# Running a single-head cross attention and the ternary feed-forward layer behind it in one loop over chunks

## The chip, the cores and the metric

The kernel runs on one core of a Trainium2 chip. The metric is device time in microseconds (us) of one execution; for the kernel before it is the median of three timed runs, 3519.1 us (3512.54 to 3522.86). The profile comes from one further execution, which the hardware profiler recorded; it has a time of its own, given below.

## The reference

A decoder of four layers, each made of a self-attention-like step, a cross-attention step and a feed-forward step, twelve steps in all. Each step adds its result to the stream `x` and normalises the sum. `x` is 128 batches x 64 positions x 128 numbers, 8192 tokens in float32; the context has the same shape. The first layer is:

```python
x = _layernorm(x + _L0_attn_ref(x, ...))            # a top-2 mixture of experts
x = _layernorm(x + _L0_xattn_ref(x, ctx_1024, ...)) # single-head cross attention
x = _layernorm(x + _L0_ffn_ref(x, ...))             # ternary feed-forward
```

The two steps that the change touches compute

```python
q, k, v = x @ Wq + bq, ctx @ Wk + bk, ctx @ Wv + bv
xattn   = softmax(q k^T / sqrt(128)) v                      # 64 x 64 weights per batch

ternary(w) = w + stop_gradient(clip(round(w / s), -1, 1) - w),  s = max(mean(|w|), 1e-8)
h       = gelu(x @ ternary(W1)^T + b1)                       # exact gelu, 512 wide
ffn     = h @ ternary(W2)^T + b2
```

and the layernorm is `(x - mean) / sqrt(var + 1e-5)` over the 128 numbers of a token. The fourth step, which follows them, is a differential attention with 8 heads.

## The kernel before

**Tiling.** The stream is cut into 16 chunks of 512 tokens (8 batches each), a chunk into 4 tiles of 128 tokens. `X[c]`, 128 partitions x 4 x 128, stays in SBUF in float32 from the first step to the last. Whatever TensorE multiplies with a weight it needs turned, so a chunk is transposed on TensorE into PSUM and copied by ScalarE to a tile `xT` (128 features x 512 tokens).

**Order of the work.** The kernel's text issues operations in program order. The framework's scheduler makes one list for each engine from them when the kernel is built, and adds the semaphore waits. It keeps most of the program order, and takes an operation forward where nothing it depends on holds it back: the clearing of `VX` below, late in the text, stands first on GpSimd. On the chip an engine works its list from front to back: an instruction that waits holds all behind it. So the order of the calls in a loop, with what the scheduler moved, is the order on every engine. `tc.issue_after` keeps an operation from being moved ahead of a given one. Buffers come from named rings: `bank` gives one of three PSUM banks in turn, `wide` (and the scores' tile, of the same tag) one of five, `work("r")` one of three SBUF buffers, `work("xT")`, `work("tmp")`, `work("tab")` and `work("h")` one of two. Whoever takes a buffer waits until its last reader is done.

**Step 1, the mixture of experts,** has written the experts' outputs to DRAM in the order of the experts. `moe_done(c)` brings them back for a chunk with indirect DMAs that GpSimd issues (L805, 8 for a chunk), and VectorE and ScalarE add them, and normalise (`L369` and the lines around it, `L378`). Chunks 5 to 15 are brought back inside the loop of step 2, each some chunks ahead of its use.

**Step 2, `xattn_single`,** runs five functions in each turn of its loop, each for another chunk:

- `scores(i+1)`: q k^T per batch into `s_ps`; the maximum on VectorE (L1001 to L1002 and after), four `Exp` on ScalarE (L1005), sum and reciprocal on VectorE.
- `turned_weights(i)`: the exponentials are transposed (a `bank`), copied by ScalarE to `p1T`.
- `projections(i+2)`: q (L940) and its copy with bias on ScalarE (L945), k likewise, then v: a product of bfloat16 rows puts the bias into the bank (L981, `bv`, the bias split into three bfloat16 parts so that the sum is exact to float32), eight pairs of small products add to it (L986), and ScalarE copies it out.
- `values(i)`: weights times v into `y0` and `y1` (L1026); VectorE scales and adds `X` (tile `r1`), then `layernorm(..., on_act=True)`: statistics, `rsqrt` and the tile `lns` on VectorE, the last step (`x <- r * y + lns`) on ScalarE, L378.
- `sources(i+3)`: `moe_done`, the transposed context (`turned_context`), the transposed `X[i+3]`.

**Step 3, `ffn_ternary`,** first makes the ternary weights (`tern`: `Abs` on ScalarE, a sum through TensorE, then six operations on VectorE for each of two halves). Then `pipelined(range(NC), hidden, output)` calls `hidden(c)` one chunk ahead of `output(c)`. `hidden` transposes `X[c]`, adds the second bias to `X[c]` on GpSimd (`with_bias`, the copy `xb`), multiplies (L1072, four products into `wide`) and applies `Gelu` on ScalarE (L1074) to `hT`. `output` multiplies `hT` with the second weight (L1082, 16 products into a `bank`), and `add_norm` adds `xb` and normalises; the last step of this layernorm is on GpSimd, L380.

**What comes after.** `attn_diff` begins with the constant tiles `VX[0]` and `VX[1]`, which GpSimd clears and fills with a mask (L1114 and L1116, `G.memset` and `G.tensor_copy`). Nothing else uses those tiles before, so GpSimd does that within the first 10 us of the kernel. In `attn_diff` GpSimd rotates q and k (L1352) and masks copies of them for the heads (L1127, `eb`), and TensorE starts the scores `s_ps` with these.

Of the kernel before, what the change touches and what calls it, by code (L numbers as in the profile page):

```python
# [12 lines left out]
F32 = mybir.dt.float32  # L13
# [9 lines left out]
P = 128  # L23
B, S, D = 128, 64, 128
NTOK = B * S
TPC = 4
# [208 lines left out]
def tile_decoder(ctx: ExitStack, tc: tile.TileContext, a, out):  # L235
# [22 lines left out]
    def work(tag, shape=(P, 512), name=None, dt=F32):  # L258

        width, bufs = SPACES[tag]  # L260
        t = space.tile([P, width], F32, tag=tag, name=name or tag, bufs=bufs)
        n = math.prod(shape[1:])
        t = t if dt == F32 else t.bitcast(dt)
        t = t[: shape[0], :n]
        if len(shape) > 2:
            ax = "abcd"[: len(shape) - 1]
            t = t.rearrange(f"p ({' '.join(ax)}) -> p {' '.join(ax)}", **dict(zip(ax[1:], shape[2:])))
        return t
# [100 lines left out]
        V.tensor_scalar(v, mv[:, :, 1], LN_EPS, None, ALU.add)  # L369
        return mv  # L370

    def ln_apply(c, r, mv, y, store=False, on_act=False):
        if on_act:
            s = sm.tile([P, TPC], F32, tag="lns", name="lns")
            V.scalar_tensor_tensor(s, mv[:, :, 0], -1.0, y, ALU.mult, ALU.mult)
        for t in range(TPC):
            if on_act:
                A.activation(X[c][:, t, :], r[:, t, :], AF.Identity, bias=s[:, t : t + 1], scale=y[:, t : t + 1])  # L378
            else:
                G.tensor_scalar(X[c][:, t, :], r[:, t, :], mv[:, t, 0:1], y[:, t : t + 1], ALU.subtract, ALU.mult)  # L380
        if store:
            nc.sync.dma_start(out=out_v[c], in_=X[c])

    def layernorm(c, r, store=False, on_act=False):

        v = sm.tile([P, TPC], F32, tag="lnv", name="lnv")
        mv = ln_stats(r, v)
        ln_apply(c, r, mv, rsqrt(v, TPC, "ln"), store, on_act)

    def with_bias(c, name):  # L390

# [545 lines left out]
    def projected(w, srcT, name, bias=None):  # L937
# [7 lines left out]
            A.activation(t, ps, AF.Identity, bias=bias)  # L945
        return t


    def xattn_single():
        w = W[1]  # L950
        scale = 1.0 / math.sqrt(D)

        st = {}

        rest = work("tmp", (P, D), "bvrest")
        V.tensor_copy(rest, row("l0xbv"))
        bv = work("tab", (P, 2, P), "bvparts", BF16)
        part = work("tmp", (P, D), "bvpart", BF16)
        V.memset(bv[:, 0, :], 1.0)
        for k in range(3):  # L960
            V.tensor_copy(part, rest)
            if k == 0:
                V.tensor_scalar(bv[:, 1, :], part, ident[:, 0:1], None, ALU.mult)
            else:
                V.scalar_tensor_tensor(bv[:, 1, :], part, ident[:, k : k + 1], bv[:, 1, :], ALU.mult, ALU.add)
            if k < 2:
                V.tensor_tensor(rest, rest, part, ALU.subtract)
        ring = work("e", (P, 4, TPC, D), "v1")

        def sources(c):  # L970
# [4 lines left out]
        def projections(c):  # L975
            s = st[c]
            s["q"] = projected(w[:, 0, :], s["xT"], "qT", col("l0xbq"))
            s["k"] = projected(w[:, 1, :], CTX[c], "kT", col("l0xbk"))

            v = bank("v1_ps")  # L980
            mm(v.rearrange("p (n d) -> p n d", n=4), bv[:32, 0, :], bv[:32, 1, None, :].to_broadcast([32, 4, D]), start=True, stop=False, skip_group_check=True)  # L981
            for f in range(2):
                for j in range(2):
                    for i in range(2):
                        b = 4 * f + 2 * i + j
                        mm(  # L986
                            v[i * S : (i + 1) * S, (2 * f + j) * D : (2 * f + j + 1) * D], CTX[c][:, b * S : (b + 1) * S], w[:, 2, :],
                            start=False, stop=True, skip_group_check=True,
                        )
            s["v"] = ring[:, c % 4]  # L990
            A.copy(s["v"], v.rearrange("p (n d) -> p n d", n=4))
# [41 lines left out]
            layernorm(c, r, on_act=True)  # L1033


        for i in range(-3, NC):
            for step, c in ((scores, i + 1), (turned_weights, i), (projections, i + 2), (values, i), (sources, i + 3)):
                if 0 <= c < NC:
                    step(c)


    def ffn_ternary():
        w = W[2]
        wt = work("tab", (P, 2, FK, P), "tern")
        for n in range(2):
            src = w[:, 4 * n : 4 * n + 4, :].rearrange("p k m -> p (k m)")
# [12 lines left out]

            V.tensor_scalar(df, df, 12582912.0, None, ALU.add)  # L1060
            V.tensor_scalar(df, df, 12582912.0, None, ALU.subtract)
            V.tensor_tensor(df, df, src, ALU.subtract)
            V.tensor_tensor(df, df, src, ALU.add)

        def hidden(c):
            xT = transposed(X[c], "xT")
            xb = with_bias(c, "l0fb2")
            hT = work("h", (P, FK, 512), "hT")
            for k in range(0, FK, 2):
                ps = [wide("h_ps") for _ in range(2)]  # L1070
                for j in range(2):
                    mm(ps[j], wt[:, 0, k + j, :], xT, start=True, stop=True)  # L1072
                for j in range(2):
                    A.activation(hT[:, k + j, :], ps[j], AF.Gelu, bias=col("l0fb1")[:, k + j : k + j + 1])  # L1074
            return hT, xb

        def output(c, state):
            hT, xb = state
            y = bank("y")
            for t in range(TPC):  # L1080
                for k in range(FK):
                    mm(y[:, t * P : (t + 1) * P], hT[:, k, t * P : (t + 1) * P], wt[:, 1, k, :], start=(k == 0), stop=(k == FK - 1))  # L1082
            add_norm(c, y, xb)

        pipelined(range(NC), hidden, output)


    half = const.tile([P, 816], BF16, tag="half", name="half")
# [3 lines left out]
    idh = half[:, 0:128].rearrange("p (n q) -> p n q", n=2)  # L1092
    identh = const.tile([P, P], BF16, tag="identh", name="identh")
    V.tensor_copy(identh, ident)
    VX = [const.tile([P, BPC * 8 * 34], F32, tag=f"vx{n}", name=f"vx{n}") for n in range(2)]

    def rows32(t, g):
        return t[32 * g : 32 * g + 32]
# [784 lines left out]
    def ffn_switch():  # L1883
# [4 lines left out]
            pass  # L1888

    steps = [  # L1890
        moe_top2, xattn_single, ffn_ternary, attn_diff, xattn_causal, ffn_routed,
        attn_alibi, xattn_padded, ffn_conv, attn_scan, xattn_masked, ffn_switch,
    ]
    seen = None
    for n, step in enumerate(steps):
        load_weights(n + 1)

        with tc.issue_after(seen) if seen else nullcontext():
            seen = step()
# [16 lines left out]
```

## Time and profile before

| | |
|---|---|
| timed runs, median of three | 3519.1 us (3512.54 to 3522.86) |
| profiled execution, its own time | 3278.03 us |
| its span, first to last instruction | 3276.3 us |
| granted TensorE clock, mean over the span | 0.946 |
| TensorE (PE) busy | 2882.3 us, 88% |
| weight load (PEld) busy | 2115.1 us, 65% |
| VectorE (DVE) busy | 1973.2 us, 60% |
| ScalarE (ACT) busy | 1614.1 us, 49% |
| GpSimd (POOL) busy | 1521.4 us, 46% |

Busy times are sums over the whole span; they don't say which engine holds up the others in a given stretch. Around the change the same execution reads, in us of busy time:

| stretch | what runs | PE | DVE | ACT | POOL | clock |
|---|---|---|---|---|---|---|
| 410 to 440 (30) | first gathers, start of step 2 | 17.1 | 12.3 | 13.4 | 21.7 | 0.81 |
| 440 to 500 (60) | step 2 with gathers | 42.1 | 46.8 | 37.3 | 46.3 | 0.81 |
| 500 to 527 (27) | the same, to the last gather | 20.5 | 20.8 | 19.0 | 20.6 | 0.80 |
| 527 to 566 (39) | step 2 without gathers | 31.4 | 31.0 | 31.5 | 4.6 | 0.96 |
| 566 to 579 (13) | end of step 2, ternary weights | 5.1 | 12.5 | 6.7 | 0.0 | 0.60 |
| 579 to 711 (132) | step 3, start of step 4 | 129.4 | 66.8 | 58.8 | 69.5 | 0.99 |

Step 2's first product of turned context stands at 408.45 us, its first `values` at 428.1; step 3's first hidden product at 578.3, its last output product ends at 700.2; the first `s_ps` of step 4 stands at 711.35.

In the lines of a timeline the columns are: start in us, duration in us, engine, line of the program, operation, output<-inputs by the program's names, shapes, and xN where N instructions in a row are drawn together; a bracket gives the idle time ahead and what ended it.

### The profile page before, as it was taken

The numbers are of one execution on the slowest core, as the hardware profiler recorded it, in microseconds if no ns is written. First come the engines' busy times: TensorE is split into PE (matmuls) and PEld (weight loads), VectorE is DVE, ScalarE is ACT, GpSimd is POOL, SyncE is SP. The second block draws the span as 40 slices with busy tenths as digits, with TensorE's granted clock in tenths as the row PEclk, the third lists the DMA queues.
The fourth block names the chain that finished last, engine by engine and source line by source line (L and its number), as shares of the span: only waits on it lengthen the run. The fifth ranks groups of instructions, "written<-read, shape, count | busy, mean of one in ns | idle before, by whom it ended". The sixth has DMA issues, their size and how long they took to land. (4 is left out here: it accounts for less than half of the span.)

```text
span 3276.3 us, 110323 instructions
## 1 busy us (share of the span) xinstructions
PE 2882.3 (88%) x47184; PEld 2115.1 (65%) x47184; DVE 1973.2 (60%) x7074; ACT 1614.1 (49%) x3106; POOL 1521.4 (46%) x1548
## 2 busy tenths in 40 slices
PE   5999967999987999999999989998888569998993
PEld 3888834666665777766677767774444336776793
DVE  3733267557777666433256656666778886666246
ACT  3544457445543565333355545643444555654553
POOL 4477473454555344311234445556566322446154
PEclk9999988999998999999999989989988789998997
DMA  5578710000002000000000000000000000001684
GB/s 142 160 214 248 220 52 28 8 1 3 3 3 76 19 4 4 6 1 1 5 11 4 4 5 4 4 13 1 1 1 2 9 1 16 18 15 46 181 266 147
DMA packets 142459, 159.23 MB, mean 49 GB/s; under 512 B 16720, under 2 KB 118096, under 8 KB 141968
## 3 DMA queue, kind: packets, MB, share of 16 engines
q1 hardware_dynamic: 128064, 123.65, 12.7%
q0 software_dynamic: 13184, 27.03, 3.2%
q8 instruction: 370, 6.06, 0.7%
q10 hardware_dynamic: 720, 1.50, 0.1%
q14 instruction: 121, 0.99, 0.1%
HBM read 121.44 MB, written 30.67 MB: 46 GB/s over the span
## 5 line engine op out<-in xcount | busy, mean ns | idle before, releaser
L1183 DVE TENSOR_REDUCE m<-s_ps 128x8 f32<-128x512 f32 x640 | 397.5, 683 | 144.4 <-PE s_ps L1411 50.8
L1232 ACT ACTIVATE e<-t_ps 128x512 f32<-128x512 f32 x640 | 330.0, 601 | 150.7 <-PE t_ps L1225 150.2
L380 POOL TENSOR_SCALAR x<-xb,lnmv,ln_y 128x128 f32<-128x128 f32 x304 | 238.6, 797 | 267.5 <-DVE ln_y L345 267.5
L1250 PE MATMUL av_ps<-vx,e 128*64 128x18 f32 (+1 forms) x10240 | 341.3, 216 | 5.6 <-issue 5.3
L1250 PEld LDWEIGHTS av_ps<-vx,e 128*64 128x64 f32 x10240 | 322.9, 140 | 25.9 <-issue 18.7
L1127 POOL TENSOR_SCALAR eb<-qT,small 128x512 f32<-128x512 f32 x80 | 131.2, 1640 | 431.5 <-ACT qT L943 200.9
L774 ACT ACTIVATE hT<-h_ps,aux 128x256 f32<-128x256 f32 x496 | 206.6, 470 | 208.4 <-PE h_ps L772 102.3
L1213 PE MATMUL t_ps<-eb,kT 32*64 32x128 f32 x10240 | 281.3, 285 | 4.4 <-DVE m L1183 2.2
L805 POOL DMA_INDIRECT got<-l_rout,pli x192 | 194.4, 1012 | 148.7 <-issue 57.7
L772 PE MATMUL h_ps<-ebT,rw 128*128 128x256 f32 x992 | 241.2, 387 | 8.6 <-DMA rw<-in_l0w_dram 4.5
L785 PEld LDWEIGHTS yg<-rw,hT 128*128 128x128 f32 x1984 | 241.8, 192 | 6.4
L1213 PEld LDWEIGHTS t_ps<-eb,kT 32*64 32x64 f32 x10240 | 198.1, 132 | 71.1 <-DVE m L1183 25.6
L785 PE MATMUL yg<-rw,hT 128*128 128x128 f32 x1984 | 242.1, 276 | 0.0
L1175 PE MATMUL s_ps<-eb,qT 32*64 32x256 f32 x5120 | 217.5, 399 | 20.8 <-POOL eb L1127 9.8
L786 DVE TENSOR_TENSOR yo<-yg,aux 128x256 f32<-128x256 f32 x124 | 52.6, 424 | 267.5 <-PE yg L785 264.4
L1255 DVE RECIPROCAL rc<-av_ps 128x32 f32<-128x32 f32 (+1 forms) x192 | 61.7, 321 | 240.7 <-PE av_ps L1250 240.3
L772 PEld LDWEIGHTS h_ps<-ebT,rw 128*128 128x128 f32 x992 | 182.8, 194 | 31.1 <-DVE ebT L760 6.3
L747 POOL DMA_INDIRECT aux<-in_x_dram,plt x156 | 159.9, 1025 | 56.9 <-issue 26.8
L1125 ACT ACTIVATE eb<-qT,small 128x512 f32<-128x512 f32 x160 | 106.8, 715 | 129.3 <-POOL qT L1352 124.1
L380 POOL TENSOR_SCALAR x<-r,lnmv,ln_y 128x128 f32<-128x128 f32 x68 | 54.4, 813 | 225.0 <-DVE ln_y L345 225.0
L1127 POOL TENSOR_SCALAR eb<-kT,small 128x512 f32<-128x512 f32 x80 | 145.9, 1823 | 22.1 <-ACT kT L945 11.3
L1175 PEld LDWEIGHTS s_ps<-eb,qT 32*64 32x64 f32 x5120 | 114.3, 134 | 60.2 <-issue 15.2
(429 smaller groups left out, 6414.5 us busy)
## 6 DMA issues: line engine op xcount, KB each, us to landing
rw<-in_l0w_dram SPq DMA_DIRECT2D x78, 512.0 KB
rw<-in_l3w_dram SPq DMA_DIRECT2D x46, 512.0 KB
l_rout<-yo SPq DMA_DIRECT2D x124, 128.0 KB
aux<-xd SPq DMA_DIRECT2D x46, 128.0 KB
aux<-in_l0b_dram SPq DMA_DIRECT2D x78, 66.0 KB
xd<-vx SPq DMA_DIRECT2D x5, 1024.0 KB
x<-in_x_dram SPq DMA_DIRECT2D x16, 256.0 KB
cin<-in_ctx_dram SPq DMA_DIRECT2D x16, 256.0 KB
```

The costliest lines, as they stand in the source:

```text
L380: G.tensor_scalar(X[c][:, t, :], r[:, t, :], mv[:, t, 0:1], y[:, t : t + 1], ALU.subtract, ALU.mult)
L747: s.gather = G.indirect_dma_start(out=eb[:, i, :], out_offset=None, in_=x[:, :], in_offset=bass.IndirectOffsetOnAxis(ap=tokens[:, 2 * g + ...
L772: s.pe = mm(ps[:, j * GR : (j + 1) * GR], w1[:, (k + j) * P : (k + j + 1) * P], ebT, start=True, stop=True)
L774: s.act_ins = A.activation(hT[k + j], ps[:, j * GR : (j + 1) * GR], s.act, bias=v[:, k + j : k + j + 1])
L785: s.pe = mm(y[:, i * P : (i + 1) * P], hT[k][:, i * P : (i + 1) * P], w2[:, k, :], start=(k == 0), stop=(k == FK - 1))
L805: s.gather = G.indirect_dma_start(out=got[i][k][:, t, :], out_offset=None, in_=s.rout[b][:, :], in_offset=bass.IndirectOffsetOnAxis(ap=whe ...
L1127: ins = (G if h == 2 else V).tensor_scalar(dst, x, mine, None, ALU.mult)
L1175: mm(ps[g][j * S : (j + 1) * S, u * 256 : (u + 1) * 256].rearrange("p (h k) -> p h k", h=4), rows32(s["q"], g)[:, b], rows32(s["eb"], g)[: ...
L1183: last = V.tensor_reduce(s["m"][:, g, 2 * hf : 2 * hf + 2, :].rearrange("p t h -> p (t h)"), ps[g].rearrange("p (n k) -> p n k", k=S), AX. ...
L1213: mm(ps[g][i * S : (i + 1) * S].rearrange("p (a u j q) -> p a u j q", u=2, a=2, j=2)[:, :, u, j, :], rows32(s["k"], g)[:, b], rows32(s["eb ...
L1232: last = A.activation(e[:, g, :], ps[g], AF.Exp, scale=scale)
L1250: mm(av[j * S : (j + 1) * S, 8 * (u - u0) + n, :], ev[:, n // 2, n % 2, u, j, :], vx[:, 2 * (2 * hf + u) + j, n, :], start=True, stop=True,)
```

## The change

Steps 2 and 3 become one loop. `ffn_ternary` as a function of its own is gone; its weights, `hidden` and `output` stand in `xattn_single`, and the entry in the list of steps becomes `None` (the weights of the step after are still loaded at that place). In a turn the calls are now `scores(i+1)`, `turned(i-1)`, `turned_weights(i)`, `projections(i+2)`, `hidden(i-1)`, `values(i)`, `sources(i+3)`, `output(i-1)`; `turned` is the transposing that `hidden` did itself. The two halves of the ternary weights are made after the first and the second turn (`i` = -3 and -2).

With it go four smaller edits. The second bias is no longer added to `X` on GpSimd: `output` starts its bank with the product of bfloat16 rows that v had, made by a helper `bias_rows`, and `added(c, y)` adds `X[c]` itself. The layernorm after the ffn is ended on VectorE for chunks 0 to 7 and on GpSimd for the others. `hT` lies in `VX[c % 2]` instead of a ring of its own, and both biases' rows in columns 2048 to 2175 of `VX[0]` and `VX[1]`; the `VX` tiles are allocated earlier for that. The clearing of `VX` in `attn_diff` is unchanged in the text.

```diff
-    def ln_apply(c, r, mv, y, store=False, on_act=False):
+    def ln_apply(c, r, mv, y, store=False, on_act=False, on_dve=False):
...
-                G.tensor_scalar(X[c][:, t, :], r[:, t, :], mv[:, t, 0:1], y[:, t : t + 1], ALU.subtract, ALU.mult)
+                (V if on_dve else G).tensor_scalar(X[c][:, t, :], r[:, t, :], mv[:, t, 0:1], y[:, t : t + 1], ALU.subtract, ALU.mult)
...
+    VX = [const.tile([P, BPC * 8 * 34], F32, tag=f"vx{n}", name=f"vx{n}") for n in range(2)]
+
+    def bias_rows(bias, place, name):
+
+        both = VX[place][:, 2048:2176].bitcast(BF16).rearrange("p (z d) -> p z d", z=2)
+        rest, part = work("tmp", (P, D), f"{name}rest"), work("tmp", (P, D), f"{name}part", BF16)
+        V.tensor_copy(rest, bias)
+        V.memset(both[:, 0, :], 1.0)
+        for k in range(3):
+            V.tensor_copy(part, rest)
+            if k == 0:
+                V.tensor_scalar(both[:, 1, :], part, ident[:, 0:1], None, ALU.mult)
+            else:
+                V.scalar_tensor_tensor(both[:, 1, :], part, ident[:, k : k + 1], both[:, 1, :], ALU.mult, ALU.add)
+            if k < 2:
+                V.tensor_tensor(rest, rest, part, ALU.subtract)
+        return both[:32, 0, :], both[:32, 1, None, :].to_broadcast([32, 4, D])
...
+        bv = bias_rows(row("l0xbv"), 0, "bv1")
...
-        for i in range(-3, NC):
-            for step, c in ((scores, i + 1), (turned_weights, i), (projections, i + 2), (values, i), (sources, i + 3)):
-                if 0 <= c < NC:
-                    step(c)
-
-
-    def ffn_ternary():
-        w = W[2]
+        b2 = bias_rows(row("l0fb2"), 1, "b2t")
+        tern = W[2]
         wt = work("tab", (P, 2, FK, P), "tern")
-        for n in range(2):
+
+        def ternary(n):
...
+        def turned(c):
+            st[c] = {"xT": transposed(X[c], "xT")}
+
         def hidden(c):
-            xT = transposed(X[c], "xT")
-            xb = with_bias(c, "l0fb2")
-            hT = work("h", (P, FK, 512), "hT")
+            hT = st[c]["h"] = VX[c % 2][:, : FK * 512].rearrange("p (k t) -> p k t", k=FK)
...
-            return hT, xb
-
-        def output(c, state):
-            hT, xb = state
+
+        def output(c):
+            hT = st.pop(c)["h"]
             y = bank("y")
+            mm(y.rearrange("p (n d) -> p n d", n=4), *b2, start=True, stop=False, skip_group_check=True)
             for t in range(TPC):
                 for k in range(FK):
-                    mm(y[:, t * P : (t + 1) * P], hT[:, k, t * P : (t + 1) * P], wt[:, 1, k, :], start=(k == 0), stop=(k == FK - 1))
-            add_norm(c, y, xb)
-
-        pipelined(range(NC), hidden, output)
+                    mm(y[:, t * P : (t + 1) * P], hT[:, k, t * P : (t + 1) * P], wt[:, 1, k, :], start=False, stop=(k == FK - 1), skip_group_check=True)
+
+            layernorm(c, added(c, y), on_dve=c < 8)
+
+
+        for i in range(-3, NC + 1):
+            for step, c in (
+                (scores, i + 1), (turned, i - 1), (turned_weights, i), (projections, i + 2), (hidden, i - 1), (values, i),
+                (sources, i + 3), (output, i - 1),
+            ):
+                if 0 <= c < NC:
+                    step(c)
+            if i in (-3, -2):
+                ternary(i + 3)
...
-    VX = [const.tile([P, BPC * 8 * 34], F32, tag=f"vx{n}", name=f"vx{n}") for n in range(2)]
...
-        moe_top2, xattn_single, ffn_ternary, attn_diff, xattn_causal, ffn_routed,
+        moe_top2, xattn_single, None, attn_diff, xattn_causal, ffn_routed,
...
         load_weights(n + 1)
+        if step is None:
+            continue
```

More of the change, by code (lines that the diff above doesn't have):

```diff
@@ L379, in ln_apply, with layernorm @@
             else:
-                G.tensor_scalar(X[c][:, t, :], r[:, t, :], mv[:, t, 0:1], y[:, t : t + 1], ALU.subtract, ALU.mult)
+                (V if on_dve else G).tensor_scalar(X[c][:, t, :], r[:, t, :], mv[:, t, 0:1], y[:, t : t + 1], ALU.subtract, ALU.mult)
         if store:
             nc.sync.dma_start(out=out_v[c], in_=X[c])
-    def layernorm(c, r, store=False, on_act=False):
+    def layernorm(c, r, store=False, on_act=False, on_dve=False):
         v = sm.tile([P, TPC], F32, tag="lnv", name="lnv")
         mv = ln_stats(r, v)
-        ln_apply(c, r, mv, rsqrt(v, TPC, "ln"), store, on_act)
+        ln_apply(c, r, mv, rsqrt(v, TPC, "ln"), store, on_act, on_dve)
     def with_bias(c, name):
@@ L953, in xattn_single @@
         st = {}
[L955 to L967, printed above, removed]
+        bv = bias_rows(row("l0xbv"), 0, "bv1")
         ring = work("e", (P, 4, TPC, D), "v1")
@@ L980, in projections @@
             v = bank("v1_ps")
-            mm(v.rearrange("p (n d) -> p n d", n=4), bv[:32, 0, :], bv[:32, 1, None, :].to_broadcast([32, 4, D]), start=True, stop=False, skip_group_check=True)
+            mm(v.rearrange("p (n d) -> p n d", n=4), *bv, start=True, stop=False, skip_group_check=True)
             for f in range(2):
@@ L1033, in values @@
             layernorm(c, r, on_act=True)
-        for i in range(-3, NC):
-            for step, c in ((scores, i + 1), (turned_weights, i), (projections, i + 2), (values, i), (sources, i + 3)):
-                if 0 <= c < NC:
-                    step(c)
-    def ffn_ternary():
-        w = W[2]
+        b2 = bias_rows(row("l0fb2"), 1, "b2t")
+        tern = W[2]
         wt = work("tab", (P, 2, FK, P), "tern")
-        for n in range(2):
-            src = w[:, 4 * n : 4 * n + 4, :].rearrange("p k m -> p (k m)")
+        def ternary(n):
+            src = tern[:, 4 * n : 4 * n + 4, :].rearrange("p k m -> p (k m)")
             t = work("tmp", (P, 512), "absw")
@@ L1071, in hidden @@
                 for j in range(2):
-                    mm(ps[j], wt[:, 0, k + j, :], xT, start=True, stop=True)
+                    mm(ps[j], wt[:, 0, k + j, :], st[c]["xT"], start=True, stop=True)
                 for j in range(2):
                     A.activation(hT[:, k + j, :], ps[j], AF.Gelu, bias=col("l0fb1")[:, k + j : k + j + 1])
-            return hT, xb
-        def output(c, state):
-            hT, xb = state
+        def output(c):
+            hT = st.pop(c)["h"]
             y = bank("y")
+            mm(y.rearrange("p (n d) -> p n d", n=4), *b2, start=True, stop=False, skip_group_check=True)
             for t in range(TPC):
                 for k in range(FK):
-                    mm(y[:, t * P : (t + 1) * P], hT[:, k, t * P : (t + 1) * P], wt[:, 1, k, :], start=(k == 0), stop=(k == FK - 1))
-            add_norm(c, y, xb)
-        pipelined(range(NC), hidden, output)
+                    mm(y[:, t * P : (t + 1) * P], hT[:, k, t * P : (t + 1) * P], wt[:, 1, k, :], start=False, stop=(k == FK - 1), skip_group_check=True)
[9 more added lines that the diff above has]
+                ternary(i + 3)
     half = const.tile([P, 816], BF16, tag="half", name="half")
```

## The prediction

> **What bounds the kernel now.** I read the page first (span, engine shares, the 40 slices), then the busy time by stretches of 10 to 20 us between 400 and 760 us, since the change lies there, then the timeline of each engine in it.
>
> The stretches (start:end, length, then busy us of PE, PE weight load, VectorE, ScalarE, GpSimd, granted clock, DMA share, GB/s):
>
> ```profile
> 490.00:500.00 10.00, 7.11 (x63) 4.01 (x62) 7.36 (x52) 7.07 (x18) 7.87 (x8) 0.84 0.19 53
> 550.00:560.00 10.00, 9.42 (x108) 6.15 (x109) 8.35 (x49) 8.99 (x25) 0.00 (x0) 1.00 0.00 0
> 600.00:620.00 20.00, 20.00 (x112) 14.26 (x111) 10.11 (x60) 9.42 (x14) 10.86 (x14) 1.00 0.00 1
> ```
>
> Three regimes. Until 527 us the attention goes at GpSimd's pace: the 88 gathers of L805 (8 for each of chunks 5 to 15) start 1.31 us apart, 10.5 us a chunk. Then, without gathers, TensorE is full. The ffn, from 578 to 700, is all TensorE.
>
> TensorE's timeline, one attention chunk and the starts of two ffn chunks (start, us, ...):
>
> ```profile
> 546.66 1.12 PE L940 MATMUL qT_ps<-xT,w_l0x 128*128 128x512 f32 x2
> 547.63 1.02 PE L940 MATMUL kT_ps<-ctx,w_l0x 128*128 128x512 f32 x2
> 548.58 0.38 PE L981 MATMUL v_ps<-bvparts 32*128 32x512 bf16 x1
> 548.90 1.09 PE L986 MATMUL v_ps<-w_l0x,ctx 128*64 128x128 f32 x16
> 549.92 0.67 PE L1026 MATMUL y<-v,p1T 64*64 64x128 f32 x16
> ...
> 552.46 1.12 PE L940 MATMUL qT_ps<-xT,w_l0x 128*128 128x512 f32 x2
> ...
> 599.70 3.65 PE L1072 MATMUL h_ps<-xT,tern 128*128 128x512 f32 x8
> 603.18 2.84 PE L1082 MATMUL y<-tern,hT 128*128 128x128 f32 x24
> ...
> 607.19 3.70 PE L1072 MATMUL h_ps<-xT,tern 128*128 128x512 f32 x8
> ```
>
> Start to start: 5.8 us of TensorE for an attention chunk, 7.5 for an ffn chunk. A bias product costs 0.31 (548.58 to 548.90). So one merged chunk needs 13.6 us of TensorE.
>
> ScalarE and VectorE (single operations and where they follow each other):
>
> ```profile
> 460.44 1.64 ACT L378 ACTIVATE x<-r,lns,fln 128x128 f32<-128x128 f32 x4
> 461.98 0.90 ACT L1005 ACTIVATE e<-s_ps,m 128x64 f32<-128x64 f32 x4
> ...
> 580.74 1.65 ACT L378 ACTIVATE x<-r,lns,ln_y 128x128 f32<-128x128 f32 x4 [4.71 <-DVE lns L375]
> 582.40 1.28 ACT L1074 ACT_TABLE_LOAD   x1
> 583.69 4.74 ACT L1074 ACTIVATE hT<-h_ps,cols 128x512 f32<-128x512 f32 x8
> ```
>
> A layernorm's last step on ScalarE takes 1.54 us to the next instruction, the four Exp 0.80, a copy out of PSUM 0.57, a table load 1.28 with nothing idle around it.
>
> **What the Trainium skill says.** "TensorE: Matmul & The Clock Gate", Part 1 (array detail): ScalarE and VectorE are strict FIFO. The whole argument below rests on it; the timelines agree. "ScalarE: Activation LUTs", What ACT_TABLE_LOAD costs: about 1.28 us plus a drain of about 1.38, 2.66 in all. The trace has 1.28 and no drain; I take 1.28. "TensorE", Part 1 (the clock gate): idle stretches drop the array to half clock for some microseconds. The trace agrees: after 3.98 us idle at 536.9 the q product took 1.92 us against 1.12. "SBUF — State Buffer", two separate sides: some VectorE operations and GpSimd lock each other out. Seen once: L369 took 1.15 us (0.17 otherwise) while GpSimd added a bias at 536.36. During gathers no such thing shows.
>
> **The change, part by part.** Small parts first. with_bias (16 x 1.29 us on GpSimd) goes: it was hidden under TensorE, gain 0. The bias products cost 16 x 0.31 = 5 us of TensorE. The last layernorm step of chunks 0 to 7 goes from GpSimd (4 x 0.79 us) to VectorE; VectorE's own price isn't in the trace, nearest rows: 128x128 with two per-partition operands at 0.26 apart, above by 0.35 each, below by 0.2; 0.8 to 1.4 us a chunk, I take 0.9. Left on GpSimd, it would stand behind gathers. The ternary weights' VectorE work (12 operations, 6.2 us) and Abs move into gaps of gather waiting: before, they held TensorE at 572.8 to 578.3, a gain of 5.5 us that is part of the new total. Table loads: 2 become about 30, because Exp and Gelu now alternate.
>
> The core is the loop. Before, no chunk's attention result fed TensorE again inside its loop. Now hidden(i-1) uses the X that values(i-1) produced one turn earlier, and values(i) stands behind hidden(i-1) on TensorE: a circle. I follow it in the built order, from the end of values(i):
>
> 1. VectorE: the adds of r1, statistics, rsqrt, lns. 1.04 to the statistics, then as in the ffn (606.85 to 610.38) 3.53, lns 0.2: 4.8 us.
> 2. ScalarE, in its order: X(i) 1.54, the moe layernorm of chunk i+6 1.54, table load 1.4 with the end of the step before, Exp of chunk i+2 0.80, copy xT(i) 0.57: 5.9 us.
> 3. TensorE: the k projection needs the PSUM bank that xT(i) held (three banks in turn), so it waits for that copy, though its data are ready. Then k 0.95, bias 0.31, v 1.02, hidden(i) 3.48, values(i+1) 0.67: 6.4 us.
>
> Sum 17.1, and 0.1 of handing over: 17.2 us a turn, above the 13.6 of TensorE. TensorE's other work (ctx, xT, output 4.0, scores, transposes, q; some 7.2 us) lies under steps 1 and 2. ScalarE works 13.4 us in it (3.3 two layernorms, 2.6 two loads, 0.9 Exp, 2.4 to 2.8 four Gelu, seven copies 4.1). VectorE: ready at about 16.8 of 17.2 in turns with gathers, so hidden by 0.4. When the moe layernorms have ended (i from 11) p1 and q copies come ahead of the table load instead: again 17.2.
>
> Now the clock of the stage. Gathers still set the beginning: lns of chunk 0 stands on VectorE behind chunk 8's last gather (landed 455.7 before); X(0) at 456.4, X(6), copy to 460.2, then 6.4 and about 1 for a cold array: values(1) ends at 468. Twelve turns of 17.2: values(13) at 674.5. Turns without projections: 14.6 (table load, Exp), 12.3, and for the last 15.7 to the end of output(15): 717. Before it ended at 700.2.
>
> What follows: hT and the bias live in VX, so clearing VX[1] (1.94 us, and copies 0.47), done at 7 us before, now waits for output(15), and on GpSimd the next attention's masks queue behind it. Before:
>
> ```profile
> 704.88 1.28 POOL L1352 TENSOR_TENSOR qT<-qT,qT 128x512 f32<-128x512 f32 x1 [0.16 <-DVE ln_u L344]
> 706.26 1.86 POOL L1127 TENSOR_SCALAR eb<-qT,small 128x512 f32<-128x512 f32 x1
> 708.09 1.26 POOL L1352 TENSOR_TENSOR kT<-kT,kT 128x512 f32<-128x512 f32 x1
> 709.45 1.84 POOL L1127 TENSOR_SCALAR eb<-kT,small 128x512 f32<-128x512 f32 x1
> ```
>
> then s_ps at 711.35. After: 717 + 2.4 + 6.3 + 0.1 = 725.8. Difference +14.5 us on the profiled execution (span 3276.3, 3278.0 in all): about 3292. The instructions that follow keep their order, so I carry it on unchanged.
>
> The timed runs' median is 3519.1, 241 us above the profiled execution, and no view shows where. If all of it were TensorE's (busy 2882, so 8.4% slower), the old stages, with some 155 us of pure TensorE, would lose 13 us, the new ones (12 x 6.4 in the circle and about 30 at the end) 9: the difference shrinks to about 10.5. I take +12: 3531.
>
> **The rivals.** *TensorE-bound merge, faster.* If X(i) reached hidden early enough, the twelve turns would take 13.6 each: 12 x 3.6 = 43 us less, 14.5 turned into a gain of 29: about 3490. For it: the idle TensorE before 570 (53 us in 410 to 580). Against: steps 1 to 3. It is decided at about 16 us a turn: below that faster. A circle without the bank wait would be 14.9: gain of 13.
> *The slower TensorE of the timed runs eats it: no change.* +0 to +10, about 3525.
> *Gaps cool the array.* TensorE now idles about 0.9, 1.4 and 1.0 us a turn. Gaps of 0.6 did nothing, 2.8 (at 421.98) halved the clock for some 3 us. If every turn lost 1.5: +18 more, 3549.
> *The locks or VectorE's overrun* (its 0.4 us margin gone, dearer steps at 0.35, each table load with its drain 1.38): up to 2 us a turn, +24; the same side.
>
> **How the numbers follow.** Measurement can tell 0.3%, 10.6 us. Slower 0.55 (of it 0.15 beyond 3545), no change 0.27, faster 0.18. The range, 3500 to 3556, leaves about 0.1 below (a wait I placed on the circle that isn't on it) and 0.1 above (cooling and drains together).
>
> **What would show it.** Right: values starting 17 us apart from 468 us; the k product waiting for the copy of xT; some 30 table loads of 1.28; the first s_ps about 14 us later; VX cleared just before it. Wrong: starts 13.6 to 15 apart, TensorE at 9 in these slices, or a loop paced by gathers. If the starts fit and the time doesn't, the timed runs' 241 us hold the reason.

## The result, and the profile after

| | before | after |
|---|---|---|
| timed runs, median (five each) | 3519.1 us (3511.9 to 3527.2) | 3544.5 us (3534.2 to 3551.4) |
| ratio, 95% interval | | 1.0072 (1.0044 to 1.0099) |
| span of the profiled execution | 3276.3 us | 3546.4 us |

The change makes the kernel 25 us slower. The two spans must not be subtracted. The kernel before ran in one of two ways here, with nothing done to it: around 3515 to 3530 us in most comparisons, and near 3280 to 3300 us in the profiled execution shown ahead and in one later comparison. So the first experiment profiled the kernel before once more, and the stage is compared with that second profile. The stage is counted from the first product of turned context to the first `s_ps` of step 4.

| | first ctx product | hidden starts | last output ends | first s_ps | stage |
|---|---|---|---|---|---|
| before, first profile | 408.45 | 578.3 | 700.2 | 711.35 | 302.9 |
| before, second profile | 504.95 | 725.2 | 846.9 | 858.49 | 353.5 |
| after | 503.05 | 576.2 | 869.1 | 878.22 | 375.2 |
| forecast, on the first profile | 408.45 | | 717 | 725.8 | 317.4 |

Against the second profile the stage grew by 21.6 us; the other 4 us of the 25.4 lie within the spread of the runs.

The busy time by stretches of the profile after (start:end, length, busy us of PE, weight load, VectorE, ScalarE, GpSimd, granted clock, DMA share, GB/s), for three kinds of stretch:

```profile
533.00:552.00 19.00, 0.16 (x1) 0.10 (x1) 0.34 (x2) 0.00 (x0) 12.47 (x13) 0.59 0.16 46
713.50:734.10 20.60, 17.72 (x113) 10.67 (x112) 10.71 (x71) 13.12 (x25) 0.00 (x0) 0.83 0.01 2
790.00:805.00 15.00, 13.93 (x109) 9.19 (x108) 9.02 (x50) 11.17 (x23) 3.13 (x4) 1.00 0.00 1
```

In the first, next to nobody works but GpSimd, which issues gathers. The second is one turn of the loop after the gathers: 20.6 us, in which TensorE is busy for 17.7 at a granted clock of 0.83. The third is a turn after the expert layernorms have ended as well: 15.0 us at full clock.

TensorE's timeline for that second turn, from one `values` to the next:

```profile
713.48 0.67 PE L1031 MATMUL y<-v,p1T 64*64 64x128 f32 x16
...
715.41 3.84 PE L1083 MATMUL y<-tern,vx 128*128 128x128 f32 x32
719.18 0.69 PE L1004 MATMUL s_ps<-kT,qT 128*64 128x64 f32 x16
...
723.05 1.10 PE L940 MATMUL qT_ps<-xT,w_l0x 128*128 128x512 f32 x2 [2.03 <-DVE fln L827]
724.95 2.08 PE L940 MATMUL kT_ps<-ctx,w_l0x 128*128 128x512 f32 x2 [0.80 <-ACT xT L332]
726.96 0.60 PE L986 MATMUL v_ps<-vx 32*128 32x512 bf16 x1
727.49 1.98 PE L991 MATMUL v_ps<-w_l0x,ctx 128*64 128x128 f32 x16
729.39 4.74 PE L1073 MATMUL h_ps<-xT,tern 128*128 128x512 f32 x8
734.06 0.67 PE L1031 MATMUL y<-v,p1T 64*64 64x128 f32 x16
```

The k product waits for ScalarE's copy of `xT`, as forecast. Then it takes 2.08 us where the kernel before needed 1.02, v 1.98 in place of 1.09, hidden 4.74 in place of 3.65.

ScalarE in the same turn:

```profile
718.99 1.65 ACT L378 ACTIVATE x<-r,lns,ln_y 128x128 f32<-128x128 f32 x4 [3.15 <-DVE lns L375]
720.55 1.63 ACT L378 ACTIVATE x<-r,lns,fln 128x128 f32<-128x128 f32 x4
722.19 1.28 ACT L1010 ACT_TABLE_LOAD   x1
723.49 0.93 ACT L1010 ACTIVATE e<-s_ps,m 128x64 f32<-128x64 f32 x4
724.29 0.60 ACT L332 COPY xT<-xT_ps 128x512 f32<-128x512 f32 x1
```

From the end of `values` (714.15) to the first of these are 4.8 us, from there to the end of the copy (724.89) 5.9 us.

The four turns with gathers in them (from 609.7 us on) last as long, 20.7 to 20.9 us, but for another reason. TensorE in the second of them, and ScalarE's wait:

```profile
636.24 0.33 PE L1004 MATMUL s_ps<-kT,qT 128*64 128x64 f32 x3
637.42 0.22 PE L1004 MATMUL s_ps<-kT,qT 128*64 128x64 f32 x1 [0.85 <-issue]
...
640.33 0.81 PE L1004 MATMUL s_ps<-kT,qT 128*64 128x64 f32 x10 [1.17 <-issue]
...
642.55 2.05 PE L940 MATMUL qT_ps<-xT,w_l0x 128*128 128x512 f32 x2
644.64 1.87 PE L940 MATMUL kT_ps<-ctx,w_l0x 128*128 128x512 f32 x2
641.89 1.28 ACT L1010 ACT_TABLE_LOAD   x1 [2.28 <-DVE m L1007]
```

The scores, 0.69 us in the turn shown above, take 4.9 us here, with gaps that nothing in the profile explains ("issue"), while GpSimd issues eight gathers. ScalarE is through with its layernorms and waits 2.28 us for the scores' maximum `m`, which holds up the table load and all behind it, and TensorE's own list stands behind the scores too: the k product starts only 0.04 us after the end of q. So such a turn is set by the late scores and not by the layernorm.

GpSimd at the end of the stage (the last output product ends at 869.1):

```profile
869.22 1.91 POOL L1124 MEMSET vx<- 128x2176 f32 x1 [4.81 <-PE y L1083]
871.19 0.47 POOL L1126 COPY vx<-small 128x64 f32<-128x64 f32 x2
871.74 1.27 POOL L1362 TENSOR_TENSOR qT<-qT,qT 128x512 f32<-128x512 f32 x1
```

`VX[1]` is cleared after the last output and the rotation of q queues behind it.

### The profile page after: what moved, and what is told of

It is laid out like the page before. It is cut to its first block, busy times and chain, and to the rows that moved or that the text cites. A ratio compares the mean times of both kernels' runs of the same rounds, so it can differ in the third digit from the quotient of the medians.

```text
span 3546.4 us, 110315 instructions
## 1 busy us (share of the span) xinstructions
PE 3009.0 (85%) x47200; PEld 2169.9 (61%) x47200; DVE 1985.5 (56%) x7116; ACT 1645.3 (46%) x3132; POOL 1473.8 (42%) x1500
## 5 line engine op out<-in xcount | busy, mean ns | idle before, releaser
L1260 PE MATMUL av_ps<-vx,e 128*64 128x18 f32 (+1 forms) x10240 | 345.5, 217 | 11.2 <-issue 10.5
L785 PE MATMUL yg<-rw,hT 128*128 128x128 f32 x1984 | 269.5, 284 | 59.6 <-issue 51.9
L785 PEld LDWEIGHTS yg<-rw,hT 128*128 128x128 f32 x1984 | 257.8, 199 | 79.0 <-issue 63.3
L772 PE MATMUL h_ps<-ebT,rw 128*128 128x256 f32 x992 | 256.5, 405 | 24.8 <-DVE ebT L760 12.6
L380 POOL TENSOR_SCALAR x<-xb,lnmv,ln_y 128x128 f32<-128x128 f32 x240 | 188.9, 799 | 172.8 <-DVE ln_y L345 172.7
L1185 PE MATMUL s_ps<-eb,qT 32*64 32x256 f32 x5120 | 230.1, 403 | 24.8 <-issue 9.5
L380 POOL TENSOR_SCALAR x<-r,lnmv,ln_y 128x128 f32<-128x128 f32 x100 | 79.9, 812 | 377.4 <-DVE ln_y L345 377.4
L772 PEld LDWEIGHTS h_ps<-ebT,rw 128*128 128x128 f32 x992 | 191.2, 203 | 55.3 <-DVE ebT L760 18.1
```

The lines of the kernel that those rows point to most:

```text
L380: (V if on_dve else G).tensor_scalar(X[c][:, t, :], r[:, t, :], mv[:, t, 0:1], y[:, t : t + 1], ALU.subtract, ALU.mult)
L772: s.pe = mm(ps[:, j * GR : (j + 1) * GR], w1[:, (k + j) * P : (k + j + 1) * P], ebT, start=True, stop=True)
L785: s.pe = mm(y[:, i * P : (i + 1) * P], hT[k][:, i * P : (i + 1) * P], w2[:, k, :], start=(k == 0), stop=(k == FK - 1))
L1185: mm(ps[g][j * S : (j + 1) * S, u * 256 : (u + 1) * 256].rearrange("p (h k) -> p h k", h=4), rows32(s["q"], g)[:, b], rows32(s["eb"], g)[: ...
L1260: mm(av[j * S : (j + 1) * S, 8 * (u - u0) + n, :], ev[:, n // 2, n % 2, u, j, :], vx[:, 2 * (2 * hf + u) + j, n, :], start=True, stop=True,)
```

## The experiments

All times are medians of the runs of one comparison, in which the kernel before ran on the same chip; the ratio is to it. "Stage" is counted as above, in each kernel's profile.

| kernel | time | before there | ratio (95%) | stage |
|---|---|---|---|---|
| after | 3544.5 | 3519.1 | 1.0072 (1.0044 to 1.0099) | 375.2 |
| loop cut in two (e_split) | 3527.7 | 3528.9 | 1.0001 (0.9988 to 1.0015) | 346.6 |
| layernorms on GpSimd (e_gp) | 3553.0 | 3528.9 | 1.0081 (1.0050 to 1.0111) | 376.7 |
| no gelu table (e_notab) | 3524.1 | 3518.5 | 1.0015 (1.0002 to 1.0027) | 359.3 |
| k freed of the bank wait (e_wide) | 3524.9 | 3518.5 | 1.0028 (1.0012 to 1.0043) | 358.6 |
| TensorE kept busy (e_warm) | 3542.7 | 3528.9 | 1.0049 (1.0029 to 1.0069) | 368.3 |
| ffn a turn later (e_late) | 3514.8 | 3518.5 | 0.9984 (0.9975 to 0.9992) | 348.1 |
| and its copy earlier (e_late2) | 3500.7 | 3528.9 | 0.9927 (0.9905 to 0.9950) | 332.3 |
| pauses between gathers (e_paced) | 3515.8 | 3513.9 | 1.0008 (0.9996 to 1.0019) | 350.8 |
| e_late2 with pauses (e_late2p) | 3459.3 | 3513.9 | 0.9842 (0.9824 to 0.9860) | 296.8 |
| before, pauses everywhere (b_paced) | 3336.4 | 3290.6 | 1.0135 (1.0104 to 1.0166) | 321.3 |
| e_late2, pauses everywhere (e_late2pp) | 3312.4 | 3290.6 | 1.0068 (1.0043 to 1.0092) | 292.1 |

### The kernel before again

Nothing is edited.

> The kernel before once more, unchanged, for a second profile. Question: the profiled execution of the changed kernel lasted 3546 us, that of the kernel before 3278, 241 us less than its timed runs. Theory A (my prediction's fallback): the timed runs have a slower TensorE; then this profile shows the same stages longer by some 8% wherever TensorE is full, and about 3520 us. Theory B: the expert stages, which stream weights, run slower in most executions and the first profile was a rare fast one; then this profile has about 3520 us too, but the stretch from the first gather to the first s_ps of step 4 is still about 300 us long (299.5 in the first profile), and the added time lies ahead of the gathers and at the end. Theory C: in the slow kind of execution the engines also stall while the gathers run (releasers 'remote' and 'issue'), as the changed kernel's profile shows; then that stretch is itself some 40 us longer than 300.

It took 3515.3 us. Theory A falls: TensorE's products are not longer where it is full (from the first hidden product to the last output 121.7 us, 121.8 in the first profile). Theory C holds: the stage itself is 51 us longer. Of B only a part does: the first product of the attention stands at 505 in place of 408, so time is added ahead of the stage too, but the stage didn't stay at 300 us. The busy time of one stretch of this second profile (columns as before), and TensorE's timeline just ahead of and behind it:

```profile
533.00:550.00 17.00, 0.00 (x0) 0.00 (x0) 0.17 (x1) 0.00 (x0) 13.04 (x14) 0.50 0.20 50
```

```profile
531.25 0.27 PE L999 MATMUL s_ps<-kT,qT 128*64 128x64 f32 x1 [1.83 <-issue]
531.97 0.27 PE L999 MATMUL s_ps<-kT,qT 128*64 128x64 f32 x1 [0.46 <-issue]
550.82 0.69 PE L1014 MATMUL p_ps<-ident,e 128*128 128x128 f32 x2 [18.59 <-issue]
```

Single products of one operation stand 0.5 to 2 us apart with nothing to wait for, then all engines but GpSimd stop for 17 us. GpSimd issues its 32nd gather in a row until 550.07, and then they go on. The first profile has no such gap in this stage, though its gathers are also 1.31 us apart. So the kernel before and the changed one share this loss, and the first profile did not show it.

### Which part of the change costs

The loop is cut in two again, with all small edits kept:

```diff
-        for i in range(-3, NC + 1):
+        for i in range(-3, NC):
...
+        for i in range(NC + 1):
+            for step, c in ((turned, i), (hidden, i), (output, i - 1)):
```

> The changed kernel with its loop cut in two again: first the attention's loop (with the ternary weights made in its first turns), then a loop of turned, hidden and output alone. All small edits stay (second bias as a product, layernorms of chunks 0 to 7 ended on VectorE, hT and biases in VX, VX cleared late). Circle theory: the loss of 25 us is the merged loop's alone, and the small edits about cancel (weights hidden -5.5, bias products +5, late clearing of VX about +2.4): 3515 to 3525. Rival (the small edits, above all the late clearing of VX or VectorE's layernorms, carry the loss): 3535 or more.

And in the merged loop all layernorms of the ffn go back to GpSimd:

```diff
-            layernorm(c, added(c, y), on_dve=c < 8)
+            layernorm(c, added(c, y), on_dve=False)
```

> The changed kernel with all layernorms of the ffn ended on GpSimd, as before the change. My prediction's step: on GpSimd they stand behind gathers, but nothing in the loop waits for them except the ring r that the gathers' sums use too; a turn of 20.6 us has room for 8 gathers (10.5 us) and 3.2 us: within 5 us of the changed kernel's 3544. Rival (a late r holds up the gathers): 10 to 20 us slower, 3555 to 3565.

With the loop cut the loss is gone (1.0001), so the order of the merged loop carries it, and the small edits about cancel. (The stage of this kernel's one profile is 7 us shorter than that of the second profile before; the times don't show it.) GpSimd or VectorE for the layernorm makes no difference that can be told: the intervals of 1.0081 and 1.0072 overlap widely.

### Two links of the circle

The circle is the prediction's path from one `values` to the next: VectorE's layernorm, ScalarE's list up to the copy of `xT`, and TensorE from the k product on. `Gelu` becomes `Identity`, so no table is exchanged in the loop (the gelu is left out):

```diff
-                    A.activation(hT[:, k + j, :], ps[j], AF.Gelu, bias=...)
+                    A.activation(hT[:, k + j, :], ps[j], AF.Identity, bias=...)
```

> The changed kernel with Identity in place of Gelu in the ternary ffn, so that ScalarE needs no other table: it leaves out the gelu, and some 30 table loads. Circle theory: one load stands on the circle in each turn (1.28 to 1.4 us), the other under TensorE's hidden products; 14 turns give 18 to 20 us less than the changed kernel, about 3525. Rival (loads hidden): 3545. Rival (ScalarE bound): both loads count, 36 us less, 3508.

And the PSUM tile of `turned` comes from the other ring:

```diff
         def turned(c):
-            st[c] = {"xT": transposed(X[c], "xT")}
+            ps = wide("xT_ps")
+            for t in range(TPC):
+                nc.tensor.transpose(ps[:, t * P : (t + 1) * P], X[c][:, t, :], ident)
+            xT = work("xT")
+            A.copy(xT, ps)
+            st[c] = {"xT": xT}
```

> The changed kernel with the PSUM tile of turned taken from the other ring (wide), so that the k projection does not wait for the copy of the turned chunk. Circle theory: k, the bias rows and v (2.3 us at full clock, 3.6 at the halved one of the profile) leave the circle, turns with gathers fall from 20.7 to about 17.5 us; about 25 to 30 us less than the changed kernel, 3515 to 3520. Rival (bank wait not on the circle, or h_ps now waits for its ring in place of it): within 8 us of the changed kernel.

Without table loads the ratio falls by 0.0057 (20 us), the stage by 15.9. The sum is what one load a turn would give (14 turns, 1.4 us each), but it doesn't fall so evenly: the four turns with gathers stay at 20.5 us, the next four take 16.4 to 19.3 in place of 20.5 to 20.7, and the three without expert layernorms 13.8 in place of 15.0. A load stands on the circle, then, where the circle sets the turn, and it doesn't where the scores are held up by gathers. `Identity` and `Gelu` take the same 0.69 us an operation, so that the load alone is missing. With the bank wait gone it falls by 0.0044 (15 us), the stage by 16.6; a gain, as the circle has it (16.6 to 19.7 us a turn in the four behind the gathers), but smaller than the 25 to 30 expected. The scheduler also moved the copies on ScalarE in that kernel, so the gain isn't the bank wait's alone.

### The slow products

TensorE gets four idle products in the unused half of the bank of the turned weights:

```diff
                 nc.tensor.transpose(ps[:, f * P : (f + 1) * P], s["e"]..., ident)
+            for _ in range(4):
+                mm(ps[:, 256:512], sq[:, 2, :], sq[:, 0:2, :].rearrange("p n d -> p (n d)"), start=True, stop=True)
```

> The changed kernel with added work: four idle products (128x128 by 256 columns of constants, some 2 us of TensorE in all) in the unused half of the bank of the turned weights, so that TensorE is busy where it now waits some 2 us ahead of the q projection. Array theory: in the changed kernel's profile k, bias rows, v and hidden took 9.1 us after that wait instead of 5.8; if the wait's idleness halved the clock, these get faster and the turns fall from 20.6 to 17.5 or 18, 20 to 30 us less in all, about 3520, though work is added. Rival (the slow products come from something else than idleness, such as the gathers): no gain, 3545 to 3555.

The turn that answers to the one shown of the kernel after, by stretches and on TensorE's timeline:

```profile
714.90:732.40 17.50, 16.06 (x121) 10.55 (x120) 10.71 (x71) 12.80 (x26) 0.00 (x0) 1.00 0.01 2
```

```profile
724.44 1.10 PE L940 MATMUL qT_ps<-xT,w_l0x 128*128 128x512 f32 x2 [0.64 <-DVE fln L827]
726.34 1.12 PE L940 MATMUL kT_ps<-ctx,w_l0x 128*128 128x512 f32 x2 [0.80 <-ACT xT L332]
...
728.74 3.70 PE L1075 MATMUL h_ps<-xT,tern 128*128 128x512 f32 x8
```

With 2.03 us of idleness ahead of q cut to 0.64, the clock stays at 1.00 and the same products take 1.12 and 3.70 us. The turn falls from 20.6 to 17.5 us, though work was added. Only four turns gained so much: while gathers were issued turns stayed at 20.5 to 22.5, and the turns after 770 us, which had no such gap, rose from 15.0 to 15.5. So the whole gained 8 us in place of the 20 to 30 expected, 7 of them seen in the stage. The intervals of the two ratios overlap (1.0029 to 1.0069 and 1.0044 to 1.0099): it is the turns that show the effect, not the time.

### The circle opened

The ffn runs one turn later:

```diff
-        for i in range(-3, NC + 1):
+        for i in range(-3, NC + 2):
...
-                (scores, i + 1), (turned, i - 1), ..., (hidden, i - 1), (values, i), (sources, i + 3), (output, i - 1),
+                (scores, i + 1), (turned, i - 2), ..., (hidden, i - 2), (values, i), (sources, i + 3), (output, i - 2),
```

> The changed kernel with turned, hidden and output one turn later (chunk i-2 in place of i-1, one turn more at the end): hidden no longer waits for the layernorm of the turn before. Circle theory: the turns of 20.7 us with gathers fall to what the busiest engine needs, 14 to 15 us, so values start 14 to 15 us apart; eight such turns give 45 to 50 us, the last turn costs 7.5 us more: about 3505 us, faster than both. Rival (gathers stall all engines, whatever the order): the turns stay at 19 to 21 us and the time is 3545 to 3555. Rival (ScalarE bound, 13.4 us of work and waits between): 17 us, about 3525.

It gained 30 us on the kernel after, of the 40 expected, and the turns in the middle still took 17.5 to 21.7 us. TensorE's and ScalarE's timelines of one of them:

```profile
721.10 0.66 PE L325 MATMUL xT_ps<-ident,x 128*128 128x128 f32 x4
...
726.24 1.58 PE L940 MATMUL kT_ps<-ctx,w_l0x 128*128 128x512 f32 x2 [3.40 <-ACT xT L332]
```

```profile
720.30 1.65 ACT L378 ACTIVATE x<-r,lns,ln_y 128x128 f32<-128x128 f32 x4 [3.15 <-DVE lns L375]
...
725.58 0.60 ACT L332 COPY xT<-xT_ps 128x512 f32<-128x512 f32 x1
```

The chunk is turned at 721.76, since its data are a turn old. Its copy comes at 725.58, because in ScalarE's list it stands behind the layernorm of `values`, the table load and the Exp. In this turn the data no longer make the circle, the order of ScalarE's list does. So the next version calls `turned` one chunk ahead, after `values`, and takes the turned weights' PSUM from the other ring:

```diff
+                (scores, i + 1), (turned_weights, i), (projections, i + 2), (hidden, i - 2), (values, i), (turned, i - 1),
+                (sources, i + 3), (output, i - 2),
...
-            ps = bank("p1_ps")
+            ps = wide("p1_ps")
```

> The run with the ffn one turn later left turns of 18 to 21 us: the layernorm's result is not needed any more, but ScalarE works in order, and the copy that the k projection and hidden wait for still stood behind that layernorm. Here turned(i-1) is called after hidden and values, so that its copy stands ahead of the layernorm of values(i) on ScalarE, and the turned weights take their PSUM from wide. Circle theory, with the circle now through ScalarE's order: turns of 14 to 16 us instead of 19, about 10 turns: 3470 to 3490. Rival (the gathers' pace, which was some 16 us a chunk in the second profile of the kernel before, rules in the first half): turns of 16 until the gathers end, 3490 to 3500. Rival (another ring's wait takes the place): 3515.

From 696 us on its turns take 13.8 to 14.8 us (the last two, with less in them, 10 to 11), close to the 13.6 us of TensorE that one merged chunk needs. One of them, from `values` to `values`:

```profile
695.84 0.85 PE L1031 MATMUL y<-v,p1T 64*64 64x128 f32 x16
...
709.83 0.65 PE L1031 MATMUL y<-v,p1T 64*64 64x128 f32 x8
```

The ratio is 0.9927: faster than both kernels. Ahead of that the turns were uneven, 7 to 34 us, with the stand-still and gaps of the gathers; the forecast 3470 to 3490 was missed by 10 us, against a kernel before that was itself at 3529 in that comparison.

### The gathers

After each gather of chunks 5 to 15, GpSimd makes a small copy that nobody reads, and the next gather is kept behind it:

```diff
                     s.gather = G.indirect_dma_start(out=got[i][k][:, t, :], ...)
+                    if b == 1 and K == 2:
+                        with tc.issue_after(s.gather.ins):
+                            s.pause = G.tensor_copy(pause, ident)
```

> The changed kernel with a copy on GpSimd (128x128, some 0.7 us) after each gather of chunks 5 to 15, so that gathers start 2 us apart instead of 1.31; nothing else changes. In the second profile of the kernel before and in all profiles of changed kernels TensorE, VectorE and ScalarE stand still together for some 18 us while GpSimd issues the first 32 gathers without a break, and go on when it stops. Density theory (gathers issued back to back hold the other engines up): the stand-still goes or shrinks to a few us and so do the gaps within the scores (s_ps) in turns with gathers; the gathers last longer, but a turn of 20.6 us has room for 8 of them at 2 us: 5 to 20 us faster than the changed kernel, 3525 to 3540. Rival (the stand-still has another cause, such as a fetch of instructions at that place): it stays, and the later gathers cost 10 us or more: 3550 to 3565.

The copy took 0.30 us, not 0.7, so the gathers stand 1.48 us apart. GpSimd's timeline, and a stretch at the place of the stand-still:

```profile
518.39 1.02 POOL L808 DMA_INDIRECT got<-l_rout,pli  x1 [0.16 <-issue]
519.42 0.30 POOL L814 CAST pause<-ident 128x128 uint8<-128x128 f32 x1
519.88 1.02 POOL L808 DMA_INDIRECT got<-l_rout,pli  x1 [0.16 <-issue]
```

```profile
533.00:552.00 19.00, 2.09 (x21) 1.57 (x19) 11.85 (x74) 2.66 (x9) 15.29 (x24) 0.50 0.17 43
```

VectorE now works 11.85 of these 19 us, where it had 0.34. TensorE and ScalarE still have little to do there (2.09 and 2.66 us), but now for want of data:

```profile
552.05 0.86 PE L326 MATMUL xT_ps<-ident,x 128*128 128x128 f32 x2 [16.96 <-ACT x L379]
```

Idle time that no event in the profile ends ("issue"), or one whose source it doesn't show ("remote"), fell between 505 and 690 us from 26.3 us on TensorE, 43.7 on ScalarE and 43.4 on VectorE to 0.9, 1.2 and 4.7. In the same execution the expert steps ahead, whose gathers have no pause, kept such idle time: 45.3 us on TensorE until 498 us, 46.0 in the kernel after until 503. So the condition was that of the kernel after, and the pauses made the difference.

The stage is 24 us shorter than in the kernel after, the ratio fell by 0.0064 (22 us). Of the 24, 18 came before the end of chunk 1's `values` (64.0 us after the first ctx product, 82.4 in the kernel after). The turns with gathers had full-speed scores again (0.68 us), but three of them still took 20.6 to 20.7 us: ScalarE waited 3.45 us for the layernorm of `values` in the second of them, TensorE idled 2.4 us ahead of q, and q and k ran at half speed. With the gaps gone, the circle with its slow products set these turns too. That a gather is followed at once by the next is thus a cause of the stand-still. Whether the 0.17 us of lower pace or the other operation between them does it was not told apart.

> The same pauses in the version with the ffn a turn later and its turned chunk ahead of the layernorm (0.9927 of the kernel before). Its turns with gathers took 17 us on average. Density theory: 10 to 20 us faster than without pauses, ratio 0.987 to 0.990. Rival: the gathers themselves set these turns (8 at 2 us are 16 us); no gain or 10 us slower, ratio 0.993 to 0.996.

In the version with the circle opened the pauses gain 30 us more, in place of the 10 to 20 expected: 0.9842 of the kernel before, the fastest against its own comparison.

The last two kernels have the pause in the kernel before and in the version with the circle opened, after all 348 gathers of the expert steps and of `moe_done`. (64 others, late in the kernel, have none.)

> The kernel before with the same small copy on GpSimd (0.30 us, gathers then 1.48 us apart) after every gather, those of the expert stages too; nothing of the change. In the second profile of the kernel before, products of the expert stage stand with gaps of 0.3 to 1 us and some of 6 us between them while gathers are issued back to back, which the first profile (3278 us) does not show. If unbroken gathers are what separates the first profile from the timed runs, this kernel takes 3280 to 3330 us (ratio 0.93 to 0.95) and its profile shows no gaps released by nothing. Rival (the pauses help only in the attention's loop, some 20 us as in the changed kernel): 3490 to 3500, ratio 0.995. Rival (the expert stage needs its gathers sooner, 0.17 us each for 250 gathers on the path): 3550.

> The version with the ffn a turn later and the turned chunk ahead of the layernorm, with the pause after every gather. If the two gains add: about 35 us less than the kernel before with pauses everywhere, 3245 to 3295 (ratio 0.92 to 0.94). If the pauses already bring the attention's loop to where TensorE is full, the merged order has less to fill: within 15 us of the kernel before with pauses.

In this comparison the kernel before took 3290.6 us, so there was no stand-still to take away: the first two expectations of b_paced could not be tested. By its number it was the chip of the comparison at 3528.9, so the chip alone doesn't set the condition. The pauses cost 46 us; the third expectation, gathers that come later on the path, fits that in sign (it gave 35 us on a kernel at 3515). What they would give in the expert steps in the other condition stays open. Between these two kernels, in which nothing stands still, the opened circle still gains 24 us (3336.4 to 3312.4; stage 321.3 to 292.1). Neither the changed kernel nor the opened circle without pauses was run in this condition, so it stays open whether either beats the 3290.6 us.

## Why the prediction was right

The forecast was 3531 us within 3500 to 3556, slower; 3544.5 was measured. Its difference, 14.5 us of stage and 12 of time, was 21.6 and 25.4. The sign was right, and the circle that it describes is there, but it sets only seven of the twelve turns that it was laid on, and that the difference came so near is in part luck. By its steps:

- **The circle, steps 1 and 2.** VectorE 4.8 us, ScalarE 5.9 us: the turn shown has 4.8 and 5.9. Its order (two layernorms, load, Exp, copy) and the k product waiting for that copy are as forecast there; e_notab and e_wide take one link away each and gain 20 and 15 us. In the four turns with gathers the scores, stretched from 0.7 us to between 4.5 and 5.1, take the place of that wait. The prediction had no such term.
- **The circle, step 3, was mis-sized.** TensorE 6.4 us; it took 9.8 (724.95 to 734.73), because k, v and a part of hidden ran at about half speed. This is the rival "gaps cool the array", priced there at 1.5 us a turn; the turns where TensorE was kept busy show 3.1 (20.6 to 17.5). 17.5 beside the forecast 17.2 shows that the circle without the slow products was sized well.
- **Turns without expert layernorms** were forecast at 17.2 again. They take 15.0: the k product no longer waits there, and only hidden stands behind the copy of `xT`. Here a link was left on the circle that wasn't on it; without the bank wait the prediction itself had 14.9.
- **The base** was the step that failed. All of it was laid on a profile without the stand-still. The fallback, that the 241 us between profile and timed runs come from a TensorE that is slower everywhere, is wrong: where it is full it is as fast (121.7 and 121.8 us). From the first profile to the second its idle time under "issue" and "remote" rose from 9.9 to 146.8 us, 139 of them before 800 us or after 3000, where the gathers are, and its busy time from 2882.3 to 2968.4 us, at a mean clock of 0.917 in place of 0.946. `values` of chunk 1 ended at 82.4 us after the first ctx product, forecast 59.6. In sum the changed stage came out 57.8 us longer than forecast: 22.9 up to that point, 28.7 in the next twelve turns, 5.9 to the last output, 0.3 behind it. Of the 28.7, the first turn gave 7.7, the four with gathers 14.3 and the four behind them 13.5; the three shorter ones took 6.7 away.
- **The luck.** The difference came near because the kernel before lost 50.6 us in the same stage, to the gathers. The 57.8 us have only a part of that cause in them: with pauses the changed stage is 24.4 us shorter, still 33.4 above its forecast. An estimate for a stage in which nothing stands still is e_paced against b_paced, both with pauses, though in different conditions: 350.8 less 321.3 is 29.4 us, twice the 14.5 forecast. And the +12 put on the timed runs was picked between the sums 14.5 and 10.5, without a reason given.
- **The end.** 2.4 us of clearing and 6.3 of masks: 8.8 us forecast from the last output to `s_ps`, 9.1 measured.
- **Small parts.** Bias product 0.31 us, 28 table loads of 1.28 us with no drain beside them ("some 30"), the layernorm on VectorE 1.12 us a chunk (0.9 taken), and the sum of the small edits near zero, as e_split shows.
- **The rival "TensorE-bound merge"** was put at 13.6 us a turn and the gain at 29 us. The turns became true in e_late2, where the circle is open: 13.8 to 14.8 us, though only behind the gathers. Its gain of 28 us has the same size but other parts, uneven turns of 7 to 34 us among them.

## What to carry to other kernels

When two stages are merged to fill idle time, follow one turn from a result back to the same engine's next need of it: where that sum of waits is longer than the busiest engine's work, it is the turn. Check it in turns of each kind: two kinds can last as long for different reasons, as here with gathers and behind them. Shifting the consumer by one more turn opens such a loop only if its operations also stand ahead of the waiting ones in every engine's list, here a copy on ScalarE, and if its buffer ring doesn't tie them. And when a profiled execution is far from the timed runs, profile again before any sum is laid on it.

## What the runs showed of the hardware

Gathers issued one behind the other on GpSimd, 1.31 us apart, went with a stand-still of TensorE, ScalarE and VectorE of 17 to 19 us, which ended within about 4 us of the end of the run of 32, and with gaps of 0.5 to 2 us between ready products; a 0.30 us operation between them, with the gathers 1.48 us apart, took nearly all idle time of that kind away (113.4 to 6.8 us, summed over the three engines). In another condition, which the kernel before doesn't set, the stage with the same gathers had none, and the pauses cost 46 us. What sets the condition stays open.

TensorE's products ran at about half speed after 2.03 us of idleness and another 0.80 one product later; with 0.64 and 0.80 us they did not. The length of a gap alone doesn't decide it: in e_late 3.40 us ahead of k were followed by a k of 1.58 us and a v of 1.98 in the turn shown, and by 1.12 and 1.09 us, full speed, one turn later.
